# Operands moved to PSUM, and 44 tiles' rows fetched one by one by two DMA queues, in an edge-attention kernel

## The chip, the cores and the metric

One core of one Trainium2 chip runs the kernel. The metric is the device time of one execution in microseconds: 2950.45 us is the median of three runs of the kernel before (2945.25 to 2961.28). Engines are named as in the profile: PE (TensorE, matmuls), PEld (its weight loads), DVE (VectorE), ACT (ScalarE), POOL (GpSimd), SP (SyncE). SP, ACT and POOL also start DMA transfers; "SPq" is SP's instruction queue.

## What is computed

A graph layer with 6250 nodes, 206250 edges sorted by target node, 128 features in 8 heads of 16, all in float32:

```python
Qh = (h @ WQ).reshape(N, H, D)
Kh = (h @ WK).reshape(N, H, D)
Vh = (h @ WV).reshape(N, H, D)
Eh = (edge_attr @ WE).reshape(-1, H, D)
...
score = jnp.einsum('ehd,ehd,ehd->eh', Kh[src], Qh[dst], Eh) * inv_sqrt_d
score = jnp.exp(jnp.clip(score, -5.0, 5.0))
msg = Vh[src] * score[:, :, None]
wV = jax.ops.segment_sum(msg, dst, num_segments=N)
Z = jax.ops.segment_sum(score, dst, num_segments=N)
h_out = wV / (Z[:, :, None] + 1e-06)
...
x = _layernorm(x + h_out.reshape(N, H * D), axis=-1)
```

The costly part is `Kh[src]` and `Vh[src]`: for each edge one row of K and V of a node anywhere in the graph.

## The kernel before, in words

**Tiles and batches.** Edges are cut into 1612 tiles of 128, and four tiles make a batch (`B`, L25). A table `kv` in DRAM holds one row of 1 KB, K beside V, for each node (`table`, L169). The loop at L372 takes one batch per step, in three stages that lie one step apart: `stage_a(b)`, `stage_b(b-1)`, `stage_c(b-2)`. From step 12 on (`XB`) the order of the instructions on each engine is the written one (`manual_schedule`, L374).

**Gathers.** For each tile POOL issues one indirect DMA, which reads 128 rows of `kv` at the node numbers in one column of `src_sb` (`gather`, L251). The first 12 batches gather rows of `x` and project them on the chip (`project`). There are `GB` = 20 batches of gathered rows on the chip, so POOL may run ahead of the arithmetic by about that much. Sixteen tiles are not gathered by POOL: `sp_gather` (L195) lets SP fetch their rows with one DMA for each row, 128 of them spread over 23 steps (`SPN`). For this SP loads 16 node numbers into registers (L210), and then computes an address and starts a DMA for each (L214).

**Arithmetic of a batch.** DVE writes a one-hot matrix of target nodes (`stage_0`, L273: `iota_f` compared with `rel`). PE transposes it (L284) and projects the edge features (L287); ACT copies the transpose from PSUM to SBUF (L289, `onehotT`); PE multiplies it with the window's Q rows (L292). DVE then forms K times Q (L301), times E (L303), sums by head (L306) and clips (L309). ACT takes the exponential (L311) into the last 8 columns of `msg`. One step later DVE multiplies V with it (L331, both operands in SBUF), and PE adds one-hot times messages to the sums of a window (L346). The operands of L273 are both in SBUF as well; L301 and L303 each have one in PSUM.

**Once in 11 tiles.** A new window needs its Q rows: a matmul at L239 and an ACT copy at L241 (`qw`); the finished window's sums go to SBUF by an ACT copy at L356 (`sum`). Once in 33 tiles `finish` (L317) adds windows (L319, copy at L326, `fin`), and a layer norm follows, one DVE instruction at each `fill()`; its store is SP's (L514).

**SP's queue.** In order: one load of edge features for each 8 tiles (512 KB, L226, 6 buffers), the single rows of L214, the loads of `x` (L485) and the stores (L514). Eight semaphores serve the DMAs of SP and ACT in turn; a DMA waits until the one before it on its semaphore has landed.

[...]

Of the kernel before, what the change touches and what calls it, by code (L numbers as in the profile page):

```python
# [9 lines left out]
I32 = mybir.dt.int32  # L10
AF = mybir.ActivationFunctionType
# [20 lines left out]
SPN = 23                       # batches from one tile of SP's rows to the next  # L32
AHEAD = 2                      # batches that the one-hot matrices run ahead
EB = 6                         # edge loads on the chip
SPL = 6                        # batches from the last of its rows to its use
SLAG = 2                       # batches from an output's arithmetic to its store
SPT = list(range(NT - 29, B * (XB + SPN + SPL), -(SPN * B + 1)))[::-1]   # SP's tiles, one DMA a row
SPR = 16                       # indices that SP loads at once


def cut_batches():
    out, t = [], 0
    while t < NT:
        if t in SPT:
            k = 1
        elif t >= NT - TAIL:
            k = 2 if NT - t > 3 else 1
        else:
            stops = [s for s in SPT if s > t] + [NT - TAIL]
            k = min(B, stops[0] - t)  # L50
        out.append(range(t, t + k))
        t += k
    return out

# [17 lines left out]
def edge_attention(ctx: ExitStack, tc: tile.TileContext, x, xT, srcT, srow, dstT, lo, eaT,  # L72
# [23 lines left out]
    shift = cp.tile([P, 3 * P], F32, name="shift")    # shift[i, c] = (c == i + 128)  # L96
# [5 lines left out]
    with ExitStack() as fast:  # L102
# [13 lines left out]
        def relative(a, b):  # L116
            """rel = dst - window start, of tiles a to b"""
            while a < b:
                g = a // G
                if a % G or b - a < G:  # L120
                    e = min(b, (g + 1) * G)
                    nc.vector.tensor_tensor(rel[:, a:e], dst_sb[:, a:e],
                                            lo_sb[:, g:g + 1].to_broadcast([P, e - a]), op=ALU.subtract)
                else:
                    e = b - (b - a) % G
                    k = (e - a) // G
                    nc.vector.tensor_tensor(
                        rel[:, a:e].rearrange("p (g t) -> p g t", t=G),
                        dst_sb[:, a:e].rearrange("p (g t) -> p g t", t=G),
                        lo_sb[:, g:g + k, None].to_broadcast([P, k, G]), op=ALU.subtract)  # L130
# [24 lines left out]
        gp = fast.enter_context(tc.tile_pool(name="gather", bufs=GB))  # L155
        ep = fast.enter_context(tc.tile_pool(name="edges", bufs=EB))
# [33 lines left out]
        batches = cut_batches()  # L190
        nbat = len(batches)
        manual = []
        sp_rows, sp_idx, xbs, stores, norms, pending, ready = {}, {}, {}, [], [], [], []

        def sp_gather(b):  # L195
            """SP's share of the gathers: the rows of tile SPT[i], spread over the batches before it"""
            for i, t in enumerate(SPT):
                at = SPB[i]
                a, e = at - SPN - SPL, at - SPL
                if b == a - 2:  # L200
                    sp_idx[t] = wp.tile([1, P], I32, name="spidx")
                    nc.sync.dma_start(sp_idx[t], srow[:, i * P:i * P + P])
                if not a <= b < e:
                    continue
                r0, r1 = (P * (v - a) // (e - a) for v in (b, b + 1))
                if b == a:
                    sp_rows[t] = wp.tile([P, 1, 2 * D], F32, name="sprows")
                for r in range(r0, r1):
                    if r % SPR == 0:
                        sp_vals[:] = nc.values_load_multi_w_load_instructions(  # L210
                            sp_idx[t][0:1, r:r + SPR], engines=(mybir.EngineType.SP,),
                            min_val=0, max_val=N - 1,
                            skip_runtime_bounds_check_because="src holds node numbers")[1]
                    nc.sync.dma_start(sp_rows[t][r:r + 1, 0, :], kv[ds(sp_vals[r % SPR], 1), :])  # L214

        SPB = [next(b for b, ts_ in enumerate(batches) if ts_[0] == t) for t in SPT]
        sp_vals = []
# [27 lines left out]
        def gather(b):  # L245
            if batches[b][0] in SPT:
                return sp_rows.pop(batches[b][0])
            rows, f = (x, D) if b < XB else (kv, 2 * D)
            g = gp.tile([P, B, 2 * D], F32, name="kvrows")
            for i, t in enumerate(batches[b]):  # L250
                nc.gpsimd.indirect_dma_start(  # L251
                    out=g[:, i, :f], out_offset=None, in_=rows,
                    in_offset=bass.IndirectOffsetOnAxis(ap=src_col(t), axis=0))
            return g

        def project(g, n):
            """K and V rows in the place of gathered x rows"""
# [5 lines left out]
            for i in range(0, n, 2):  # L263
                k = min(2, n - i)
                pk = psT.tile([P, 2, 2 * D], F32, name="kvps", tag="oT")
# [4 lines left out]
        def stage_0(b):  # L270
            t0, n = batches[b][0], len(batches[b])
            oh = wp.tile([P, B, P], F32, name="onehot", bufs=AHEAD + 4)
            nc.vector.tensor_tensor(oh[:, :n], iota_f[:, None, :].to_broadcast([P, n, P]),  # L273
# [24 lines left out]
        def stage_b(b):  # L298
# [10 lines left out]
            nc.vector.tensor_scalar(sc[:, :n], sc[:, :n], -20.0, 20.0, op0=ALU.max, op1=ALU.min)  # L309
            m = wp.tile([P, B, MW], F32, name="msg")  # L310
# [3 lines left out]
        def add_windows(ps, q, stop):  # L314
            """add the sums of the windows that reach into block q"""
# [13 lines left out]
        def stage_c(b):  # L329
            n, g, oh, m = st8.pop(b)  # L330
# [3 lines left out]
                m[:, :n, D:, None].to_broadcast([P, n, H, DH]), op=ALU.mult)  # L334
# [26 lines left out]
        gathered = {b: gather(b) for b in range(min(XB, len(batches)))}  # L361
        for b0 in range(0, NB, KB):
# [3 lines left out]
        def fill():  # L366
            """one step of a layer norm, between the others of VectorE"""
# [4 lines left out]
        for b in range(nbat + 3):  # L372
# [6 lines left out]
            if b < nbat:  # L379
                load_chunk(batches[b][0] // CH + EB - 3)  # L380
                sp_gather(b)
# [37 lines left out]
def any_order(ctx, tc, x, xT_sb, srcT, dstT, eaT, wq_sb, we_sb, iota_f, out, kv, qtab):  # L419
    """The same for edges in any order: each tile of edges is added to every block of nodes."""  # L420
# [68 lines left out]
def layernorm(nc, sp, agg, xb, out, q, stores):  # L489
    """agg: sums of messages and scores of 128 nodes; gives their output rows, an instruction a step"""  # L490
# [14 lines left out]
    # y = (var + eps) ** -0.5: a start from the exponent, then Newton's steps  # L505
# [50 lines left out]
```

## Time and profile before

| what | value |
|---|---|
| median of three runs | 2950.45 us |
| span of the profiled execution, first to last instruction | 2098.6 us |
| median less span | 851.9 us |
| mean granted TensorE clock in it | 0.939 |
| PE, DVE, ACT, POOL busy | 1644.2, 1480.1, 441.4, 1593.3 us |
| DMA traffic | 334.66 MB, mean 159 GB/s |
| HBM read, written | 322.27 MB, 9.60 MB |

The span is that of one profiled execution on the core; the time of the runs also holds what lies before the first and after the last instruction of the program. Busy time is summed over the span, so an engine at 76% may still be the one that all others wait for. A group's row names the line, the engine, the operation, what it writes and reads, the count, then busy time and mean duration, then the idle time of the engine just before these instructions and what ended it.

### The profile page before, as it was taken

How to read it: one execution, taken by the hardware profiler on the slowest of the kernel's cores; microseconds unless marked ns; L12 is line 12 of the kernel's file. 1: busy time of each engine (PE TensorE's matmuls, PEld its weight loads, DVE VectorE, ACT ScalarE, POOL GpSimd, SP SyncE). 2: the span in 40 equal slices, each digit the busy share in tenths (PEclk: the TensorE clock that was granted, in tenths of full speed). 3: DMA queues.
4: the chain of work that ended last, by engine and by line, in shares of the span. 5: the costliest groups of instructions: out<-in, count | busy, mean ns of one | idle time of the engine just before them, and what ended most of it. 6: DMA issues, size and time to landing. Idle time of an engine off the chain costs nothing.

```text
span 2098.6 us, 40013 instructions
## 1 busy us (share of the span) xinstructions
PE 1644.2 (78%) x12306; PEld 1561.1 (74%) x12306; DVE 1480.1 (71%) x3330; ACT 441.4 (21%) x1239; POOL 1593.3 (76%) x1602
## 2 busy tenths in 40 slices
PE   7999787877787677777788777787778777877776
PEld 6899776777777677777787676777767677777766
DVE  3598677777676676777767776767677677766676
ACT  3422121212111121211112122212212121212211
POOL 7777777777777777777777777777777777777775
PEclk9999899999999999999979999989999999899998
DMA  9555455555555455555555455545555555455542
GB/s 313 168 165 177 145 157 153 165 158 150 164 161 162 142 164 158 157 156 152 160 154 169 136 173 159 156 145 166 159 157 155 158 166 158 146 159 149 167 139 79
DMA packets 131782, 334.66 MB, mean 159 GB/s; under 512 B 32790, under 2 KB 54372, under 8 KB 131556
## 3 DMA queue, kind: packets, MB, share of 16 engines
q0 software_dynamic: 75840, 206.15, 33.3%
q1 hardware_dynamic: 54996, 125.45, 19.5%
q8 instruction: 98, 1.61, 0.3%
q14 instruction: 128, 1.05, 0.2%
q10 hardware_dynamic: 720, 0.41, 0.1%
HBM read 322.27 MB, written 9.60 MB: 158 GB/s over the span
## 4 chain that ended last, share of the span: by engine, by line
POOL 30%; DMA 23%; DVE 21%; issue 19%; PE 6%; DVEq 0%; ACT 0%; SPq 0%; POOLq 0%
POOL kvrows L251 30%; DMA kvrows<-kv,src 22%; DVE kq L301 5%; DVE kq L303 5%; DVE sc L306 4%; DVE msg L331 3%; PE agg L346 2%; PE eps L287 2%; PE qps L292 1%; DVE sc L309 1%; PE oTps L284 1%; DVE onehot L273 1%; DVE w L511 0%; PE finps L319 0%; DVEq L301 0%
## 5 line engine op out<-in xcount | busy, mean ns | idle before, releaser
L251 POOL DMA_INDIRECT kvrows<-kv,src x1548 | 1546.2, 999 | 471.7 <-issue 384.9
L346 PE MATMUL agg<-msg,onehot 128*128 128x136 f32 x3224 | 518.6, 306 | 424.2 <-DVE msg L331 389.1
L346 PEld LDWEIGHTS agg<-msg,onehot 128*128 128x128 f32 x3224 | 438.8, 204 | 481.2 <-DVE msg L331 479.6
L301 DVE TENSOR_TENSOR kq<-kvrows,qps 128x512 f32<-128x512 f32 (+1 forms) x402 | 274.4, 682 | 542.1 <-DMA kvrows<-kv,src 450.7
L292 PE MATMUL qps<-qw,onehotT 128*128 128x128 f32 x3224 | 476.9, 291 | 3.3 <-ACT onehotT L289 2.6
L287 PE MATMUL eps<-we_sb,ea 128*128 128x128 f32 x3224 | 461.5, 289 | 0.0
L287 PEld LDWEIGHTS eps<-we_sb,ea 128*128 128x128 f32 x3224 | 429.5, 207 | 0.1
L292 PEld LDWEIGHTS qps<-qw,onehotT 128*128 128x128 f32 x3224 | 405.6, 197 | 18.3 <-ACT onehotT L289 9.2
L289 ACT COPY onehotT<-oTps 128x512 f32<-128x512 f32 (+2 forms) x418 | 238.6, 571 | 644.5 <-PE oTps L284 641.3
L306 DVE TENSOR_REDUCE sc<-kq 128x32 f32<-128x512 f32 (+2 forms) x418 | 278.3, 666 | 9.4
L303 DVE TENSOR_TENSOR kq<-kq,eps 128x512 f32<-128x512 f32 (+2 forms) x418 | 278.6, 667 | 7.5
L273 DVE TENSOR_TENSOR onehot<-iota_f,rel 128x512 f32<-128x512 f32 (+2 forms) x418 | 277.4, 664 | 0.0
L331 DVE TENSOR_TENSOR msg<-kvrows,msg 128x512 f32<-128x512 f32 (+1 forms) x402 | 274.2, 682 | 4.0 <-ACT msg L311 3.9
L284 PE MATMUL oTps<-shift,onehot 128*128 128x128 f32 x1612 | 271.3, 294 | 0.0
L284 PEld LDWEIGHTS oTps<-shift,onehot 128*128 128x128 f32 x1612 | 213.8, 153 | 2.5 <-ACT kvrows L268 2.1
L311 ACT ACTIVATE msg<-sc 128x32 f32<-128x32 f32 (+2 forms) x418 | 95.9, 229 | 468.5 <-DVE sc L309 466.5
L309 DVE TENSOR_SCALAR sc<-sc 128x32 f32<-128x32 f32 (+2 forms) x418 | 82.9, 198 | 9.5
L241 ACT COPY qw<-qwps 128x128 f32<-128x128 f32 x147 | 39.2, 267 | 217.0 <-PE qwps L239 216.8
L356 ACT COPY sum<-agg 128x136 f32<-128x136 f32 x146 | 39.7, 272 | 148.1 <-PE agg L346 146.3
L319 PE MATMUL finps<-sum,shift 128*128 128x136 f32 x478 | 64.5, 283 | 0.0
L319 PEld LDWEIGHTS finps<-sum,shift 128*128 128x128 f32 x478 | 59.9, 193 | 0.0
L251 POOL DMA_INDIRECT kvrows<-x,src x48 | 46.3, 964 | 16.5 <-issue 14.3
(50 smaller groups left out, 437.5 us busy)
## 6 DMA issues: line engine op xcount, KB each, us to landing
ea<-eaT SPq DMA_DIRECT2D x201, 512.0 KB
sprows<-kv SPq DMA_DIRECT2D x2048, 1.0 KB
kvrows<-kv,src POOLq DMA_INDIRECT x1548
kv<-kvst SPq DMA_DIRECT2D x12, 512.0 KB
xb<-x SPq DMA_DIRECT2D x48, 64.0 KB
out<-h SPq DMA_DIRECT2D x48, 64.0 KB
xT_sb<-xT SPq DMA_DIRECT2D x5, 535.0 KB
kvrows<-x,src POOLq DMA_INDIRECT x48
```

The lines of the kernel that those rows point to most:

```text
L251: nc.gpsimd.indirect_dma_start(out=g[:, i, :f], out_offset=None, in_=rows, in_offset=bass.IndirectOffsetOnAxis(ap=src_col(t), axis=0))
L273: nc.vector.tensor_tensor(oh[:, :n], iota_f[:, None, :].to_broadcast([P, n, P]), rel[:, t0:t0 + n, None].to_broadcast([P, n, P]), op=ALU.i ...
L284: nc.tensor.transpose(oT[:, i, :], oh[:, i, :], ident)
L287: nc.tensor.matmul(pe[:, i, :], ea_tile(t0 + i), we_sb, start=True, stop=True)
L289: nc.scalar.copy(ohT[:, :n], oT[:, :n])
L292: nc.tensor.matmul(pq[:, i, :], ohT[:, i, :], window_q(*group_of(t0 + i)), start=True, stop=True)
L301: nc.vector.tensor_tensor(t1[:, :n], g[:, :n, :D], pq[:, :n], op=ALU.mult)
L303: nc.vector.tensor_tensor(t1[:, :n], t1[:, :n], pe[:, :n], op=ALU.mult)
L306: nc.vector.tensor_reduce(sc[:, :n], t1[:, :n].rearrange("p b (h d) -> p b h d", h=H), axis=AX.X, op=ALU.add)
L319: nc.tensor.matmul(ps, shift[:, P - s:2 * P - s], sums[k], start=i == 0, stop=stop and i == len(parts) - 1)
L331: nc.vector.tensor_tensor(m[:, :n, :D].rearrange("p b (h d) -> p b h d", h=H), g[:, :n, D:].rearrange("p b (h d) -> p b h d", h=H), m[:, : ...
L346: nc.tensor.matmul(aggs[k], oh[:, i, :], m[:, i, :], start=first and not final, stop=last)
```

## The change

Two operands move to PSUM. A new PSUM bank holds `iota_p`, a copy of `iota_f` that is made once, and `exp_p`, 32 columns for one batch of exponentials. The one-hot comparison reads `iota_p`. The exponential is taken twice by ACT, into `exp_p` and into the columns of `msg`; the product with V reads `exp_p`. For the bank, `psT` goes from two buffers to one, and the products of `project` go to `psE` and `psQ`. The exponentials move behind the next one-hot comparison in the written order, and `stage_c` is split into `messages` and the rest.

Eleven batches of four tiles are fetched row by row, in place of sixteen tiles: 336 of a batch's 512 rows by SP and 176 by ACT, spread over 33 steps that end 4 steps before the batch's own. The steps 12 to 374 hold such rows, some 10 on SP and 5 or 6 on ACT in each step; ACT's stand at the end of a step, behind its exponentials and its `sum` copy and ahead of the next step's `onehotT` copy. Node numbers are loaded once and multiplied by 1024 once, on DVE; each register load still brings 16 of them, and each DMA takes its address from a register as it is, as bytes. POOL gathers 1568 tiles (1596 before), the last of them without its padding. All batches but the last few have four tiles now (406 batches, 418 before). `GB` goes from 20 to 18, `SLAG` from 2 to 4 (steps from an output's arithmetic to its store).

```diff
-GB = 20                        # batches of gathered rows on the chip
+GB = 18
...
-SLAG = 2                       # batches from an output's arithmetic to its store
+SLAG = 4
+RN = 33
+RL = 4
+RSP = 336
+RV = 16
+RBYTES = 4 * 2 * D
...
+ROWB = list(range(XB + RN + RL, len(BATCHES) - TAIL, RN))
...
+        off_sb = ip.tile([len(ROWB), B * P], I32, name="off_sb")
...
+        def row_offsets():
+            nc.scalar.dma_start(off_sb, srow)
+            nc.vector.tensor_scalar(off_sb, off_sb, float(RBYTES), None, op0=ALU.mult)
...
-        psT = fast.enter_context(tc.tile_pool(name="psT", bufs=2, space=bass.MemoryType.PSUM))
+        psT = fast.enter_context(tc.tile_pool(name="psT", bufs=1, space=bass.MemoryType.PSUM))
...
+        psX = fast.enter_context(tc.tile_pool(name="psX", bufs=1, space=bass.MemoryType.PSUM))
+        bank = psX.tile([P, P + B * H], F32, name="bank")
+        iota_p, exp_p = bank[:, :P], bank[:, P:].rearrange("p (b h) -> p b h", h=H)
+        nc.vector.tensor_copy(iota_p, iota_f)
...
+        def single_rows(b, queue):
+            for i, at in enumerate(ROWB):
+                a, e = at - RN - RL, at - RL
                 if not a <= b < e:
                     continue
+                if at not in row_tiles:
+                    row_tiles[at] = hp.tile([P, B, 2 * D], F32, name="hwrows")
+                first, last = (0, RSP) if queue is nc.sync else (RSP, B * P)
+                r0, r1 = (first + (last - first) * (v - a) // (e - a) for v in (b, b + 1))
+                engine = mybir.EngineType.SP if queue is nc.sync else mybir.EngineType.Activation
                 for r in range(r0, r1):
+                    if (r - first) % RV == 0:
+                        vals[engine] = nc.values_load_multi_w_load_instructions(
+                            off_sb[i:i + 1, r:r + RV], engines=(engine,),
...
-                    nc.sync.dma_start(sp_rows[t][r:r + 1, 0, :], kv[ds(sp_vals[r % SPR], 1), :])
+                    queue.dma_start(row_tiles[at][r % P:r % P + 1, r // P, :].bitcast(U8),
+                                    kv_bytes[None, ds(vals[engine][(r - first) % RV], RBYTES)])
...
-            nc.vector.tensor_tensor(oh[:, :n], iota_f[:, None, :].to_broadcast([P, n, P]),
+            nc.vector.tensor_tensor(oh[:, :n], iota_p[:, None, :].to_broadcast([P, n, P]),
...
+        def weigh(b):
+            n, g, oh, sc = st8[b]
+            nc.scalar.activation(exp_p[:, :n], sc[:, :n], AF.Exp, scale=0.25)
             m = wp.tile([P, B, MW], F32, name="msg")
             nc.scalar.activation(m[:, :n, D:], sc[:, :n], AF.Exp, scale=0.25)
...
+        def messages(b):
+            n, g, oh, m = st8[b]
             nc.vector.tensor_tensor(
                 m[:, :n, :D].rearrange("p b (h d) -> p b h d", h=H),
                 g[:, :n, D:].rearrange("p b (h d) -> p b h d", h=H),
-                m[:, :n, D:, None].to_broadcast([P, n, H, DH]), op=ALU.mult)
+                exp_p[:, :n, :, None].to_broadcast([P, n, H, DH]), op=ALU.mult)
...
             if 0 <= b - 1 < nbat:
                 stage_b(b - 1)
             if 0 <= b - 2 < nbat:
-                stage_c(b - 2)
+                messages(b - 2)
             fill()
             if b + AHEAD < nbat:
                 stage_0(b + AHEAD)
+            if 0 <= b - 1 < nbat:
+                weigh(b - 1)
+            if 0 <= b - 2 < nbat:
+                stage_c(b - 2)
             fill()
+            single_rows(b, nc.scalar)
```

More of the change, by code (lines that the diff above doesn't have):

```diff
@@ L10 @@
 I32 = mybir.dt.int32
+U8 = mybir.dt.uint8
 AF = mybir.ActivationFunctionType
@@ L31 @@
 NG = (NT + G - 1) // G
-SPN = 23
 AHEAD = 2
 EB = 6
-SPL = 6
-SLAG = 2
-SPT = list(range(NT - 29, B * (XB + SPN + SPL), -(SPN * B + 1)))[::-1]
-SPR = 16
+SLAG = 4
[4 more added lines that the diff above has]
+RBYTES = 4 * 2 * D
 def cut_batches():
@@ L43, in cut_batches @@
     while t < NT:
-        if t in SPT:
-            k = 1
-        elif t >= NT - TAIL:
+        if t >= NT - TAIL:
             k = 2 if NT - t > 3 else 1
         else:
-            stops = [s for s in SPT if s > t] + [NT - TAIL]
-            k = min(B, stops[0] - t)
+            k = min(B, NT - TAIL - t)
         out.append(range(t, t + k))
@@ L53, in cut_batches @@
     return out
+BATCHES = cut_batches()
+ROWB = list(range(XB + RN + RL, len(BATCHES) - TAIL, RN))
 def group_of(t):
@@ L155, in edge_attention @@
         gp = fast.enter_context(tc.tile_pool(name="gather", bufs=GB))
+        hp = fast.enter_context(tc.tile_pool(name="rows", bufs=2))
         ep = fast.enter_context(tc.tile_pool(name="edges", bufs=EB))
@@ L188, in table @@
                 nc.sync.dma_start(kv[b * P:N], st[:N - b * P, b - b0, :])
-        batches = cut_batches()
+        batches = BATCHES
         nbat = len(batches)
         manual = []
[L193 to L202, printed above, removed]
+        xbs, stores, norms, pending, ready = {}, [], [], [], []
@@ L203, in sp_gather @@
+        row_tiles, vals = {}, {}
+        kv_bytes = kv.bitcast(U8).rearrange("n f -> (n f)")
+        def single_rows(b, queue):
+            for i, at in enumerate(ROWB):
+                a, e = at - RN - RL, at - RL
                 if not a <= b < e:
                     continue
-                r0, r1 = (P * (v - a) // (e - a) for v in (b, b + 1))
-                if b == a:
-                    sp_rows[t] = wp.tile([P, 1, 2 * D], F32, name="sprows")
+                if at not in row_tiles:
[3 more added lines that the diff above has]
+                engine = mybir.EngineType.SP if queue is nc.sync else mybir.EngineType.Activation
@@ L208, in sp_gather @@
                 for r in range(r0, r1):
[L209 to L212, printed above, removed]
+                    if (r - first) % RV == 0:
+                        vals[engine] = nc.values_load_multi_w_load_instructions(
+                            off_sb[i:i + 1, r:r + RV], engines=(engine,),
+                            min_val=0, max_val=(N - 1) * RBYTES,
@@ L213, in sp_gather @@
                             skip_runtime_bounds_check_because="src holds node numbers")[1]
-                    nc.sync.dma_start(sp_rows[t][r:r + 1, 0, :], kv[ds(sp_vals[r % SPR], 1), :])
-        SPB = [next(b for b, ts_ in enumerate(batches) if ts_[0] == t) for t in SPT]
-        sp_vals = []
+                    queue.dma_start(row_tiles[at][r % P:r % P + 1, r // P, :].bitcast(U8),
+                                    kv_bytes[None, ds(vals[engine][(r - first) % RV], RBYTES)])
         chunks, qw, aggs, sums, st8 = {}, {}, {}, {}, {}
@@ L245, in gather @@
         def gather(b):
-            if batches[b][0] in SPT:
-                return sp_rows.pop(batches[b][0])
+            if b in ROWB:
+                return row_tiles.pop(b)
             rows, f = (x, D) if b < XB else (kv, 2 * D)
@@ L250, in gather @@
             for i, t in enumerate(batches[b]):
+                k = min(P, E - t * P + 1)
+                if k < P:
+                    nc.vector.memset(g[:, i, :], 0.0)
                 nc.gpsimd.indirect_dma_start(
-                    out=g[:, i, :f], out_offset=None, in_=rows,
-                    in_offset=bass.IndirectOffsetOnAxis(ap=src_col(t), axis=0))
+                    out=g[:k, i, :f], out_offset=None, in_=rows,
+                    in_offset=bass.IndirectOffsetOnAxis(ap=src_col(t)[:k], axis=0))
             return g
@@ L264, in project @@
                 k = min(2, n - i)
-                pk = psT.tile([P, 2, 2 * D], F32, name="kvps", tag="oT")
+                pk = (psE, psQ)[i // 2 % 2].tile([P, 2, 2 * D], F32, name="kvps", tag=("eps", "qps")[i // 2 % 2])
                 for j in range(k):
@@ L309, in stage_b @@
             nc.vector.tensor_scalar(sc[:, :n], sc[:, :n], -20.0, 20.0, op0=ALU.max, op1=ALU.min)
+            st8[b] = [n, g, oh, sc]
+        def weigh(b):
+            n, g, oh, sc = st8[b]
+            nc.scalar.activation(exp_p[:, :n], sc[:, :n], AF.Exp, scale=0.25)
             m = wp.tile([P, B, MW], F32, name="msg")
@@ L327, in finish @@
             pending.append(layernorm(nc, sp, fin, xbs.pop(q), out, q, stores))
-        def stage_c(b):
-            n, g, oh, m = st8.pop(b)
+        def messages(b):
+            n, g, oh, m = st8[b]
             nc.vector.tensor_tensor(
@@ L333, in stage_c @@
                 g[:, :n, D:].rearrange("p b (h d) -> p b h d", h=H),
-                m[:, :n, D:, None].to_broadcast([P, n, H, DH]), op=ALU.mult)
+                exp_p[:, :n, :, None].to_broadcast([P, n, H, DH]), op=ALU.mult)
+        def stage_c(b):
+            n, g, oh, m = st8.pop(b)
             for i in range(n):
@@ L361, in edge_attention @@
         gathered = {b: gather(b) for b in range(min(XB, len(batches)))}
+        row_offsets()
         for b0 in range(0, NB, KB):
@@ L380, in edge_attention @@
                 load_chunk(batches[b][0] // CH + EB - 3)
-                sp_gather(b)
+                single_rows(b, nc.sync)
                 g = gathered.pop(b) if b in gathered else gather(b)
@@ L536 @@
         "srow": np.ascontiguousarray(np.concatenate(
-            [srcT[t * P:t * P + P] for t in SPT or [0]])[None]),
+            [srcT[BATCHES[b][0] * P:][:B * P][None] for b in ROWB])),
         "dstT": np.ascontiguousarray(dstT.reshape(NT, P).T),
```

## The prediction, made before the changed kernel ran

> **What bounds the kernel now.** I read first the busy times, the chain that ended last, and the costliest group.
>
> ```profile
> PE 1644.2 (78%) x12306; PEld 1561.1 (74%) x12306; DVE 1480.1 (71%) x3330; ACT 441.4 (21%) x1239; POOL 1593.3 (76%) x1602
> ...
> POOL 30%; DMA 23%; DVE 21%; issue 19%; PE 6%; DVEq 0%; ACT 0%; SPq 0%; POOLq 0%
> ...
> L251 POOL DMA_INDIRECT kvrows<-kv,src x1548 | 1546.2, 999 | 471.7 <-issue 384.9
> ```
>
> No engine is busy over 78%, yet POOL's idle time is "issue": it waits for nothing. In the timeline of POOL, the pause between two gathers is 0.30 us each time:
>
> ```profile
> 1007.94 0.95 POOL L251 DMA_INDIRECT kvrows<-kv,src  x1 [0.30 <-issue]
> 1009.19 0.95 POOL L251 DMA_INDIRECT kvrows<-kv,src  x1 [0.30 <-issue]
> 1010.45 1.13 POOL L251 DMA_INDIRECT kvrows<-kv,src  x1 [0.31 <-DVE msg L331]
> 1011.88 0.94 POOL L251 DMA_INDIRECT kvrows<-kv,src  x1 [0.30 <-issue]
> ```
>
> So POOL works end to end: its 1596 gathers start on average 1.302 us apart, from 3.7 us to 2082.2 us. Without disturbance one costs 0.95 + 0.30 = 1.25 us; the rest is stretched gathers like that of 1.13 us. In the timeline of DVE the stretched one lies on the two instructions that read two operands from SBUF:
>
> ```profile
> 1009.47 0.69 DVE L331 TENSOR_TENSOR msg<-kvrows,msg 128x512 f32<-128x512 f32 x1
> 1010.07 0.69 DVE L273 TENSOR_TENSOR onehot<-iota_f,rel 128x512 f32<-128x512 f32 x1
> ```
>
> The waits say who suffers, and the windows say what the rest could do:
>
> ```profile
> DVE kq L301 <- DMA kvrows<-kv,src: 450.7, 268, 4.2
> ACT qw L241 <- PE qwps L239: 216.8, 142, 2.9
> ACT sum L356 <- PE agg L346: 146.3, 124, 2.9
> ...
> 110.00:190.00 80.00, 77.55 (x646) 74.99 (x644) 77.74 (x180) 20.93 (x61) 61.70 (x61) 1.00 0.57 172
> ```
>
> DVE waits 450.7 us for gathered rows. From 110 to 190 us, where POOL is still ahead, DVE is busy 77.74 of 80 us and a batch takes (193.9 - 108.5) / 23 = 3.7 us, from the starts of L301 in batches 12 and 35. Later a batch takes the gathers' 4 x 1.30 = 5.2 us.
>
> **POOL's part of the change.** Of the gathers 292 take over 1.0 us; all time above 948 ns sums to 79 us. In the 277 of them after the hundredth, L273 covers 499 ns on average and L331 222 ns, against 52 and 129 ns in the short ones. Both read only one operand from SBUF afterwards. The gain lies between 0 (the overlap is chance) and 79 us. I take 60: L273 and L331 make three quarters of DVE's time in the long ones, and the layer norm's own two-operand instructions stay. DVE's rows give no reason for a price of its own: L303, with a PSUM operand, takes 686 ns, L273 683 ns. [...]
>
> Twenty-eight fewer gathers at 1.25 us give 35 us. POOL would end 95 us sooner, at 1987 us; with the 16.4 us from the last gather to the end the span is 2003, and with the 851.9 us outside it, kept as they are, 2855 us.
>
> **SP's and ACT's part.** A step of 4 tiles then has 32/33 x 4 x 1.26 = 4.9 us of POOL time (1.25 us and the 20 us of stretching left over 1568 gathers). In it SP must start 336/33 = 10.2 rows and ACT 5.3. A row costs SP now 0.41 us from start to start: 37 ns of address arithmetic, a 29 ns move and the 228 ns DMA instruction, with pauses. Afterwards it is 0.28 (DMA and its pause) to 0.34 us (the move stays). A register load took 1.23 us for 16 indices, so 0.79 us per step on SP and 0.41 on ACT; edge loads, x and stores add 0.3. SP needs 10.2 x 0.28 + 1.1 = 3.9 to 4.6 us: nearly full, with 4.9 as its limit.
>
> The eight semaphores are the doubtful point. A row lands 1.35 to 3.1 us after its issue (10th to 90th percentile; median 1.87, mean 2.10, from the semaphore records of L214), an edge load 3.97 us. The written program gives the semaphores out in turn over both queues, with ACT's rows between SP's. So no DMA starts before the eighth before it, from either queue, has landed. Before, eight rows took SP 8 x 0.41 = 3.3 us, which covered the landing, and only edge loads were waited for (29.1 us in 61 waits). Now 16.3 DMAs a step (512/33 rows, 0.5 edge loads, 0.25 for x and stores) at 1.87 us over 8 semaphores need 3.8 us with no gap at all, and while the queues alternate a pair costs 1.87 / 4 = 0.47 us.
>
> What is behind ACT's rows matters: the next step's `onehotT` copy, for which PE's L292 waits, then L346, then DVE's L301. ACT's time per step when it is not waiting for gathers: copy 0.57 + 0.09 of pauses, two exponentials at 0.23 + 0.1, `qw` with its wait for PE (216.8/142 + 0.27 = 1.8 us) and `sum` with its own (1.45 us), both 147 times in 406 batches, 1.17 us a step. That makes 2.4 us. Rows: 5.33 x 0.47 = 2.5 and 0.41 of register loads. Sum: 5.3 us a step. From both sides: 2.4 + 5.33 x 0.28 + 0.41 = 4.3 if no DMA waits (then POOL's 4.9 rules), and 3.7 + 2.9 = 6.6 if the rows stand wholly behind the work of the dense stretch. I take 5.3, because in steps with `qw` and `sum` ACT starts no row for some 3 us, in which SP gets 8 DMAs further and stops. [...]
>
> The span then: step 12 at 108 us as before, 363 steps with rows, 31 batches at 3.7 us (gathers for 18 are already there), 12 us from the last L301 to the end: 108 + 363p + 115 + 12 = 235 + 363p. No change at p = (2098.6 - 235) / 363 = 5.13. With p = 5.3 it is 2159 us, 60 more than before. Against the median: 2950.45 + 60 = 3010 us. With p = 5.8, 3192.
>
> **Edits at nothing.** The second exponential (406 x 0.23 = 93 us of ACT) is counted above. Copies of `iota_p`, the multiplication of addresses and one load lie in the first 100 us, where POOL runs ahead and needs nothing. With one `psT` buffer, and projections in `psE` and `psQ`, each of the first 12 batches may wait for a copy more: 0 to 12 x 0.6 = 7 us, hidden by the 39 us that POOL is ahead at step 12, but added to the sum where POOL doesn't bound. `SLAG` takes away SP's waits for L513 (563.6 us), of which nobody was waiting for the end. `GB` 18 only shortens a lead of 2 batches out of 20.
>
> **The rivals.**
> 1. (0.44) The forecast: the shared semaphores and ACT's order bound the steps, p = 5.3, 3010 us. For it: the landing times against 8 semaphores. Against it: ACT is busy 21%, and in before SP's waits for DMAs are small. In a part of this case, some 0.07, p lies within 0.04 of 5.13 and the time stays.
> 2. (0.36) The other side: DMA waits stay under 0.3 us a step, POOL bounds as before, with fewer and unstretched gathers: 2855 us (2832 with all 79 us). It decides when p is under 4.9: a row on ACT for 0.39 us or less (2.4 + 5.33 x 0.39 + 0.41 = 4.9).
> 3. (0.15) SP is the bound: the move stays, edge loads hold a semaphore (3.97 us against 2.5 us for a turn of eight, 1.5 us every second step) and register loads are not hidden: 4.6 + 0.75 + 0.5 = 5.85 us, 2359 us of span, 3210 us. The edge loads then come late and PE waits at L287.
> 4. (0.05) The move to PSUM does nothing, POOL bounds: only 35 us, 2915 us.
>
> **How the numbers follow.** Slower by over 0.5% (15 us, about what a measurement of this kernel can tell from no change): 0.37 of case 1 and all of case 3, 0.52. Faster: cases 2 and 4, 0.41. Same: 0.07. The time is that of case 1, 3010 us; its own range is 2950 to 3190 (p 5.13 to 5.8). The range has to take in case 2 as well: 2842 to 3190; a tenth lies below or just at its lower edge, and a tenth above, most of case 3.
>
> **What would show it.** Right: gathers of L267 with a mean near 0.96 us, but POOL waiting for buffers; ACT's rows 0.45 us or more apart; PE's L308 of the changed kernel waiting for ACT's `onehotT`; SP's row DMAs waiting for DMAs of ACT. Wrong: DVE's first product still waits for gathered rows with POOL in an even beat of 1.25 us up to about 1970 us; then case 2 holds. If gathers stay stretched on the one-hot comparison (its line 289), the PSUM part failed. An edge load that ends PE's wait at L303 is case 3. A median less span other than 852 us would break the addition.

## The result, and the profile after

The changed kernel takes 3249.24 us (median of 4 runs, 3248.23 to 3249.48). The kernel before, run beside it, takes 2947.85 us (2916.09 to 2961.28). The ratio is 1.1035, with a 95% interval of 1.0961 to 1.1109: slower by a tenth. The prediction was slower, at 3010 us with 3190 as its upper end, so the side is right and the size far too small.

The runs were made on several chips, and the kernel before takes 2883 to 2948 us on some and 2099 to 2102 us on others, so each ratio below is against the kernel before on the same chip, and each section says which kind it was.

The profiled execution of the changed kernel has a span of 3246.4 us, with 3248.23 us as its time. First the page (busy times, granted clock, costliest groups):

```profile
PE 1939.0 (60%) x12306; PEld 1828.6 (56%) x12306; DVE 1467.8 (45%) x3261; ACT 466.0 (14%) x1621; POOL 1488.9 (46%) x1574
...
PEclk6798778778778777887877887777787787787789
...
L267 POOL DMA_INDIRECT kvrows<-kv,src x1520 | 1442.3, 949 | 1725.1 <-DVE msg L353 765.7
L303 PE MATMUL eps<-we_sb,ea 128*128 128x128 f32 x3224 | 567.9, 332 | 748.8 <-DMA ea<-eaT 722.0
```

POOL worked end to end before, with 999 ns a gather. Now a gather takes 949 ns, and POOL idles 1725.1 us before these gathers. The largest part, 765.7 us, ends with DVE's `msg` (L353), that is, with the reading of a buffer of gathered rows. So the gathers became cheaper and stopped being the limit. The waits say who is late:

```profile
DVE kq L317 <- PE qps L308: 959.4, 189, 11.8
POOL kvrows L267 <- DVE msg L353: 765.7, 135, 10.8
...
PE eps L303 <- DMA ea<-eaT: 722.0, 145, 10.3
ACT onehotT L305 <- PE oTps L300: 538.8, 108, 12.8
ACT onehotT L305 <- DMA hwrows<-kv: 433.0, 183, 11.0
```

and the waits of SP's queue (us in total, times, longest):

```profile
SPq L229 <- DMA hwrows<-kv: 453.4, 290, 14.2
```

Before, DVE waited for gathered rows, and PE not for edge features (0.0 us idle before its L287). Now PE waits 722 us for edge loads (`ea`), which SP issues; DVE waits behind PE, and POOL behind DVE. And SP itself waits 453.4 us in the middle of its rows for other row transfers. A step of four tiles takes (3133.4 - 742.3) / 300 = 7.97 us, from the starts of L317 in batches 80 and 380.

The kernel's own profile of before (span 2098.6 us) came from an execution of the quicker kind. The same changed kernel, profiled where the kernel before takes 2101 us (run e15), can therefore be set against it line by line:

```profile
PE 1799.1 (66%) x12306; PEld 1717.4 (63%) x12306; DVE 1467.5 (53%) x3261; ACT 469.9 (17%) x1621; POOL 1484.9 (54%) x1574
...
PE 37%; DMA 34%; SPq 10%; DVE 6%; issue 6%; ACTq 5%; ACT 3%; DVEq 0%
DMA ea<-eaT 20%; PE qps L308 12%; DMA hwrows<-kv 12%; PE eps L303 12%; SPq L229 7%; PE agg L371 6%; ACTq L229 3%; PE finps L341 2%; SPq L225 2%; PE oTps L300 2%; DVE kq L319 1%; DVE kq L317 1%; ACT onehotT L305 1%; DVE sc L322 1%; PE qwps L252 1%
...
L267 POOL DMA_INDIRECT kvrows<-kv,src x1520 | 1438.5, 946 | 1228.7 <-DVE msg L353 518.4
```

In the chain that ended last POOL had 30%; now it has no share at all. The chain runs through edge loads (20%), PE, the single rows (12%) and the queues of SP and ACT (10% and 5%), which had none.

### The profile page after: what moved, and what is told of

Read it like the earlier page. It is cut to its first block, busy times and chain, and to the rows that moved or that the text cites. A ratio compares the mean times of both kernels' runs of the same rounds, so it can differ in the third digit from the quotient of the medians.

```text
span 3246.4 us, 45133 instructions
## 1 busy us (share of the span) xinstructions
PE 1939.0 (60%) x12306; PEld 1828.6 (56%) x12306; DVE 1467.8 (45%) x3261; ACT 466.0 (14%) x1621; POOL 1488.9 (46%) x1574
## 5 line engine op out<-in xcount | busy, mean ns | idle before, releaser
L267 POOL DMA_INDIRECT kvrows<-kv,src x1520 | 1442.3, 949 | 1725.1 <-DVE msg L353 765.7
L303 PE MATMUL eps<-we_sb,ea 128*128 128x128 f32 x3224 | 567.9, 332 | 748.8 <-DMA ea<-eaT 722.0
L303 PEld LDWEIGHTS eps<-we_sb,ea 128*128 128x128 f32 x3224 | 506.9, 239 | 787.0 <-DMA ea<-eaT 758.1
L317 DVE TENSOR_TENSOR kq<-kvrows,qps 128x512 f32<-128x512 f32 (+1 forms) x395 | 269.3, 682 | 1479.0 <-PE qps L308 959.4
L308 PE MATMUL qps<-qw,onehotT 128*128 128x128 f32 x3224 | 589.6, 341 | 306.8 <-ACT onehotT L305 154.2
L308 PEld LDWEIGHTS qps<-qw,onehotT 128*128 128x128 f32 x3224 | 529.0, 248 | 342.7 <-ACT onehotT L305 179.9
L305 ACT COPY onehotT<-oTps 128x512 f32<-128x512 f32 x406 | 236.8, 583 | 1506.8 <-PE oTps L300 538.8
L300 PE MATMUL oTps<-shift,onehot 128*128 128x128 f32 x1612 | 272.8, 296 | 130.2 <-ACT qw L254 57.0
L300 PEld LDWEIGHTS oTps<-shift,onehot 128*128 128x128 f32 x1612 | 214.8, 156 | 142.5 <-ACT qw L254 63.4
L322 DVE TENSOR_REDUCE sc<-kq 128x32 f32<-128x512 f32 x406 | 276.6, 681 | 9.1
L319 DVE TENSOR_TENSOR kq<-kq,eps 128x512 f32<-128x512 f32 x406 | 276.6, 681 | 7.4
L353 DVE TENSOR_TENSOR msg<-kvrows,bank 128x512 f32<-128x512 f32 (+1 forms) x395 | 267.4, 677 | 21.7 <-issue 11.9
L289 DVE TENSOR_TENSOR onehot<-bank,rel 128x512 f32<-128x512 f32 x406 | 275.7, 679 | 0.0
L333 ACT ACTIVATE msg<-sc 128x32 f32<-128x32 f32 x406 | 88.1, 217 | 0.1
```

The lines of the kernel that those rows point to most:

```text
L267: nc.gpsimd.indirect_dma_start(out=g[:k, i, :f], out_offset=None, in_=rows, in_offset=bass.IndirectOffsetOnAxis(ap=src_col(t)[:k], axis=0))
L289: nc.vector.tensor_tensor(oh[:, :n], iota_p[:, None, :].to_broadcast([P, n, P]), rel[:, t0:t0 + n, None].to_broadcast([P, n, P]), op=ALU.i ...
L300: nc.tensor.transpose(oT[:, i, :], oh[:, i, :], ident)
L303: nc.tensor.matmul(pe[:, i, :], ea_tile(t0 + i), we_sb, start=True, stop=True)
L305: nc.scalar.copy(ohT[:, :n], oT[:, :n])
L308: nc.tensor.matmul(pq[:, i, :], ohT[:, i, :], window_q(*group_of(t0 + i)), start=True, stop=True)
```

## The experiments

### One part at a time, where the kernel before takes 2883 us

**e1: the PSUM part alone.** The kernel before, with its 16 tiles on SP, and the two operands moved, with what goes with them: the second exponential, its place behind the next one-hot comparison, and one `psT` buffer. The main lines:

```diff
+        bank = psX.tile([P, P + B * H], F32, name="bank")
+        iota_p, exp_p = bank[:, :P], bank[:, P:].rearrange("p (b h) -> p b h", h=H)
-            nc.vector.tensor_tensor(oh[:, :n], iota_f[:, None, :].to_broadcast([P, n, P]),
+            nc.vector.tensor_tensor(oh[:, :n], iota_p[:, None, :].to_broadcast([P, n, P]),
...
-                m[:, :n, D:, None].to_broadcast([P, n, H, DH]), op=ALU.mult)
+                exp_p[:, :n, :, None].to_broadcast([P, n, H, DH]), op=ALU.mult)
```

> Only the operands in PSUM, with the order of the exponentials and one psT buffer; SP's 16 tiles as before. Theory (the rows are what costs, PSUM helps POOL): gathers at a mean of 0.95 us instead of 1.00 and 40 to 80 us less than before, a ratio of 0.973 to 0.987. Rival (the new order and the single psT buffer cost the time): a ratio of 1.03 or more, with ACT or PE waiting for the other.

Measured: 2981.87 us, ratio 1.0393 [1.0262, 1.0524]. The gathers fall to 947 ns, and the time does not:

```profile
L255 POOL DMA_INDIRECT kvrows<-kv,src x1548 | 1465.5, 947 | 1372.3 <-DVE msg L340 581.0
```

POOL idles 1372.3 us, for the most part behind DVE (581.0 us behind `msg` alone), so on this chip the gathers are not the limit, and what a cheaper gather is worth can't be read here.

**e2: the changed kernel with one batch fetched singly instead of eleven.**

```diff
-ROWB = list(range(XB + RN + RL, len(BATCHES) - TAIL, RN))
+ROWB = list(range(XB + RN + RL, len(BATCHES) - TAIL, 33 * 40))
```

> The changed kernel with one batch fetched row by row instead of eleven; POOL gathers the other 1608 tiles. Theory: without rows on SP and ACT a batch takes POOL's 5.0 us, a ratio near 0.985 to 1.0. Rival (something else of the change, SLAG or GB or PSUM, is slow): near the changed kernel's 1.10.

Measured: 2864.2 us, 0.9965 [0.9914, 1.0015], against 1.10 for eleven batches. The PSUM operands, the byte addresses and the new order of the exponentials are all in this kernel, so the loss comes with the single rows.

**e3: all 512 rows of a fetched batch on SP, none on ACT.**

```diff
-RSP = 336
+RSP = 512
```

> The changed kernel with all 512 rows of a batch on SP's queue and none on ACT's. Theory (two queues that share eight semaphores hold each other, and ACT's compute stands behind its rows): SP alone needs 15.5 rows x 0.34 us + 1.2 us of register loads + 0.3 = 6.8 us a step, less than the 7.9 us now, so faster than the changed kernel, a ratio of 0.9 to 1.02 to before. Rival (SP's own stream is the bound and ACT relieves it): slower than the changed kernel, a ratio of 1.15 or more.

Measured: 3386.53 us, 1.1784 [1.1664, 1.1904]. This is the rival's side, not the theory's. SP now issues 15.5 rows a step; its waits for other rows come to 63.5 us only, and yet PE waits 1066.8 us at L303 for edge loads. Between batches 80 and 380 SP's instructions, with the pauses of up to 0.1 us between them, take 6.7 us of a step of 8.5, more than the 4.9 us that POOL needs. So too many rows on one queue cost as well, with no row of ACT on the semaphores: SP's own issue is the limit there. That alone doesn't say which of the two holds in the changed kernel, with 10.2 rows a step.

### Where the kernel before takes 2099 us

**e4: the kernel before, profiled once.** 

> The kernel before, unchanged, for a profile beside the others of this call: its timed runs took some 2880 us, its first profile 2098.6. Theory: its span is now near its timed runs, and shows the same pauses of 5 to 9 us, in which ACT waits for PE, as the changed kernel and the two with few rows; POOL then isn't at work end to end. Rival: its span is near 2100 us again, and 800 us lie outside the span.

Measured: 2102.43 us, with a span of 2100.6. The span is near the run's time, as the theory had it, but both are near 2100 us, which neither side had: little lies outside the span.

**e5: the kernel before without single rows** (`SPT = []`), so that POOL gathers 16 tiles more.

> The kernel before with no tile fetched by SP: POOL gathers all 1612 tiles. Theory (POOL is not the bound in the timed runs, and rows on SP cost and don't help): a ratio of 0.96 to 0.995. Rival (POOL bounds, as in the first profile): 16 more gathers of 1.25 us, a ratio of 1.007 or more.

Measured: 2119.63 us, 1.0092 [1.0062, 1.0122]. Sixteen gathers at the prediction's 1.302 us are 20.8 us; the difference is 20.6. On this chip POOL is the limit of the kernel before, as its profile said.

**e6: 66 steps for a fetched batch instead of 33** (`RN = 66`: five batches, 5.1 rows a step on SP and 2.7 on ACT).

> The changed kernel with a batch's rows spread over 66 steps instead of 33: 5 batches of 512 rows, half as many rows in a step on both queues. Theory (the queues are full and hold each other on eight semaphores only at the full rate): 8.5 DMAs a step wait for little, a ratio of 0.99 to 1.02. Rival (each row costs the same, wherever it stands): 5 of 11 batches cost 2048 of 5120 rows' 0.107, a ratio of 1.03 to 1.05.

**e7: 256 rows of each of the 11 batches on SP, none on ACT**, the other two tiles gathered by POOL:

```diff
-RSP = 336
+RSP = 256
...
+            if b in ROWB:
+                g = row_tiles.pop(b)
...
+                if b in ROWB and i < RSP // P:
+                    continue
...
-            single_rows(b, nc.scalar)
```

> The changed kernel with 256 rows of a batch on SP, none on ACT, and the batch's other two tiles gathered by POOL. Theory (ACT's rows and the shared semaphores are the cost): SP needs 7.8 x 0.45 + 0.6 + 0.4 = 4.5 us a step and isn't the bound, a ratio of 0.99 to 1.02. Rival (each row costs the same): half of the rows, a ratio of 1.04 to 1.06.

Measured: e6 2019.12 us, 0.9613 [0.9587, 0.9639]; e7 2016.29 us, 0.9599 [0.9572, 0.9625]. Both are 4% faster than before, and POOL is the limit in both: e6's 1592 gathers at 1.25 us and some 25 us around them make 2015. With fewer rows, or with rows on one queue, nothing is lost.

### Again, where the kernel before takes 2948 us

**e8: the changed kernel. e9: e1's kernel. e10: e3's. e11: 44 steps for a batch** (`RN = 44`: eight batches, 7.6 rows a step on SP and 4 on ACT).

> The changed kernel once more, to be read against the kernel before on the same chip, which took 2099 us in the last call and some 2880 to 2950 us in the ones ahead of it. Where before takes about 2099 us: theory A (the shared semaphores and ACT's order bind, 5.1 us a step or more): 2090 us or more, a ratio of 1.0 to 1.05. Theory B (POOL bounds with 1568 gathers of 1.25 us): 3 + 1960 + 16 = 1980 us, a ratio of 0.943. Where before takes about 2900 us: 1.10 again.

> Only the operands in PSUM, as in e1. Where before takes about 2099 us: theory (two SBUF operands hold POOL up): 1596 gathers of 1.25 us, 2015 us, a ratio of 0.96. Rival (no gain from PSUM alone; the 4% gained by the two runs of the last call came from rows): 0.99 or more. Where before takes about 2900 us: 1.04 again.

> All 512 rows of a batch on SP, as in e3. Where before takes about 2099 us: theory (SP's stream is then the bound): 15.5 x 0.33 + 1.2 + 0.4 = 6.7 us a step, 235 + 363 x 6.7 = 2667 us, a ratio of 1.2 to 1.3. Rival (rows are hidden wherever they stand): 0.95. Where before takes about 2900 us: 1.18 again.

> The changed kernel with a batch's rows spread over 44 steps: 8 batches, 32 tiles. Where before takes about 2099 us: 1580 gathers, 3 + 1975 + 16 = 1994 us, a ratio of 0.95 if POOL bounds; above 0.96 if the queues still bind at 7.6 rows a step on SP and 4 on ACT. Where before takes about 2900 us: between 1.0 and 1.10.

Measured: e8 3255.98 us, 1.1038 [1.0949, 1.1127]; e9 3018.32 us, 1.0253 [1.017, 1.0335]; e10 3443.27 us, 1.1683 [1.1592, 1.1773]; e11 3038.13 us, 1.0289 [1.0196, 1.0382]. From one batch over eight to eleven the ratio climbs from 0.9965 (e2, on another chip) over 1.029 to 1.104, steeper at the end; the 1.029 can't be told from e9's 1.025, which has none of these rows. In e11 the waits of SP's rows for other rows are as long as in the changed kernel (499.6 us against 469.9 in e8), but PE's waits for edge loads are a third (260.4 us against 737.3): so long waits alone don't make the loss.

### Taking the two queues apart, where the kernel before takes 2101 us

**e12: SP's 336 rows kept, ACT's 176 given back to POOL** (a whole tile, and the first 48 rows of the tile that SP fetches in part):

```diff
+SKIP = 3 * P - RSP
...
+                    w = r + SKIP * (r >= 2 * P)
...
+                if b in ROWB and i < 2:
+                    continue
+                k = SKIP if b in ROWB and i == 2 else min(P, E - t * P + 1)
...
-            single_rows(b, nc.scalar)
```

> The changed kernel with ScalarE's 176 rows of each fetched batch given back to POOL (the last tile whole, and 48 rows of the tile before it), and SP's 336 rows kept. SP so issues 10.1 rows a step as before, but shares the transfers' semaphores with no row of ScalarE. Theory (SP is held back by semaphores that ScalarE's rows issued late hold, 422.8 us of 2400 in the trace of the changed kernel, and while it waits the edge loads queue behind it): SP's waits behind ScalarE's rows are gone, PE's waits for edge loads at L303 fall from 722 us to under 150, and where the kernel before takes some 2900 us the ratio is 0.98 to 1.04; where it takes 2099 POOL sets the time, 1590 gathers x 1.25 + 25 = 2013 us, ratio 0.96. Rival (the number of rows on SP alone makes the time): SP still has no rest, L303 still waits over 500 us for edge loads, and the ratio is 1.06 to 1.10 where before takes 2900 and above 0.98 where it takes 2099.

**e13: e7's kernel beside it.** 

> The kernel of e7 again, beside the others on one chip: 256 rows of each of the 11 batches on SP, 7.8 a step, none on ScalarE, the other two tiles on POOL. Where before takes some 2900 us: 0.97 to 1.03 by either theory; by the theory of shared semaphores it stands within 0.02 of e12, by the rival of row numbers it is lower than e12 by 0.03 or more. Where before takes 2099: 0.96 as in e7.

**e14: e6's kernel beside it.** 

> The kernel of e6 again, beside the others on one chip: five batches fetched singly over 66 steps each, so 5.1 rows a step on SP and 2.7 on ScalarE, semaphores still shared. Both theories: SP has time left over at this rate. Where before takes some 2900 us: 0.99 to 1.03, on the line from one batch (0.9965) to eight (1.029) and eleven (1.104). If it stands above e13 though SP issues a third fewer rows in it, the shared semaphores cost by themselves. Where before takes 2099: 0.96 as in e6.

**e15: the changed kernel beside them.** 

> The changed kernel as it is, beside the others on one chip. Where before takes some 2900 us: 1.10 again. Where it takes 2099 (not yet measured for this kernel): if POOL set the time there, 1568 gathers x 1.25 + 25 = 1985 us, ratio 0.946; by the prediction's order, 5.3 us a step over 363 steps, 2159 us, ratio 1.03; if SP sets it, 10.1 rows x 0.34 + 0.71 of register loads + 0.33 of edge loads = 4.5 us a step before any wait for a shared semaphore, and with the 1.9 us a step of such waits 6.4 us, 235 + 363 x 6.4 = 2558 us, ratio 1.22.

| run | rows a step on SP / ACT | time, us | ratio [95%] |
|---|---|---|---|
| e12 | 10.2 / 0 | 2015.52 | 0.9590 [0.9574, 0.9606] |
| e13 | 7.8 / 0 | 2016.27 | 0.9591 [0.9574, 0.9608] |
| e14 | 5.1 / 2.7 | 2018.28 | 0.9606 [0.9590, 0.9622] |
| e15 | 10.2 / 5.3 | 2749.12 | 1.3093 [1.3057, 1.3129] |

e12 and e15 differ in ACT's 176 rows of eleven batches, 1936 transfers, for which e12 has 22 gathers more on POOL; the transfers cost 734 us. SP's number of rows is not the cause by itself at this rate (e12 equals e13). Where the gathers set the time of the kernel before, the changed kernel loses 31%, three times the loss of the result. Here the expectation for SP as the limit (6.4 us a step, 2558 us) was too small too.

In e12 POOL runs without a wait again, DVE waits for gathered rows, PE no more for edge loads, and SP's rows at most for the edge loads on their semaphores. In this order the page, the waits of the engines, and the largest wait of SP's queue:

```profile
L272 POOL DMA_INDIRECT kvrows<-kv,src x1520 | 1442.1, 949 | 467.2 <-issue 368.0
```

```profile
DVE kq L322 <- DMA kvrows<-kv,src: 320.8, 209, 4.7
```

```profile
SPq L231 <- DMA ea<-eaT: 125.8, 109, 2.4
```

and in e15, the waits of the engines and of SP's queue:

```profile
DVE kq L317 <- PE qps L308: 1023.4, 291, 9.9
...
PE eps L303 <- DMA ea<-eaT: 708.8, 156, 8.4
ACT onehotT L305 <- PE oTps L300: 596.1, 141, 11.2
ACT onehotT L305 <- DMA hwrows<-kv: 592.1, 237, 11.1
```

```profile
SPq L229 <- DMA hwrows<-kv: 752.0, 495, 10.4
```

Set side by side by step (between batches 80 and 380), SP's instructions, with the pauses of up to 0.1 us between them, take 4.49 us a step in e12 and the same 4.49 us in e15. The longer pauses, in which SP waits, take 0.44 us in e12's step of 4.94 us and 2.54 us in e15's step of 7.03 us. So the whole difference is waiting. Going by the semaphore of each transfer, 988 of SP's rows in this stretch have a row of ACT just before them on their semaphore. Of these 306 waited, for 584.3 us in all: 1.95 us a step, nearly the 2.1 that e15 has above e12. In 117 cases SP arrived before ACT had begun to issue its row; these make 415.1 us, 219.0 us of it until ACT issued the row and the rest until it landed. The other 189 waited 169.2 us for a row on its way.

How the wait feeds itself shows in 17 us of e15's timeline (start, duration, engine, line, count, and the idle time before with its releaser; POOL's and DVE's lines left out):

```profile
1363.91 0.38 SPq L239 DMA_DIRECT2D ea<-eaT  x1
1364.39 16.25 SPq L229 DMA_DIRECT2D hwrows<-kv  x21
1364.89 3.64 ACTq L229 DMA_DIRECT2D hwrows<-kv  x5
...
1367.67 2.07 PE L303 MATMUL eps<-we_sb,ea 128*128 128x128 f32 x8 [6.44 <-DMA ea<-eaT]
...
1373.06 0.95 PE L300 MATMUL oTps<-shift,onehot 128*128 128x128 f32 x4
...
1374.05 0.59 ACT L305 COPY onehotT<-oTps 128x512 f32<-128x512 f32 x1 [10.18 <-PE oTps L300]
...
1377.11 1.92 ACTq L229 DMA_DIRECT2D hwrows<-kv  x5
...
1380.73 0.36 SPq L239 DMA_DIRECT2D ea<-eaT  x1
```

SP issues an edge load at 1363.91, so late that PE stands still for 6.4 us until it is there. PE's next transposes (L300) come behind that, so ACT's copy waits 10.18 us for them, and ACT's rows of that step, which stand behind the copy in ACT's queue, start at 1377.11. SP had started 17 of its 21 rows by 1373.04. Its next has the semaphore of ACT's second row, which is issued at 1377.44; SP goes on at 1378.98, 5.9 us after its last row. Behind those rows stands SP's next edge load, issued at 1380.73, again late. SP waits for ACT, ACT for PE, PE for SP's edge load: that is a loop.

What closes the loop so tightly, by this trace, is the order in which the semaphores were given out. In the written program SP loads edge features six steps ahead of their use, so SP could be some steps late at no price. But each queue issues its rows in the written order, 336 and 176 of them in 33 steps, so the step of each row can be counted. In 1086 of the 1208 places in e15 where a row of SP stands right behind a row of ACT on its semaphore, ACT's row belongs to a step that comes 5 or 6 later in the written program (1087 of 1209 in the result's trace). Above, the row of SP that waits until 1378.98 is of step 193, and the row of ACT that it waits for is of step 199; the edge load behind it, SP's of step 194, is for step 200. So SP mostly can't finish a step before ACT is five or six steps further on, and the lead of the edge loads is used up.

e14 shows that such waits need not cost anything. There SP waits for other single rows 629.8 us in all, against 752.0 in e15. But with 5 rows a step its own work is 2.3 us (between batches 20 and 340, counted as above), and its waits of 2.5 us fit into the rest of POOL's 4.9. The edge loads are on time. Two things differ from e15, though. Besides the rows being half as many a step, the row of ACT before a row of SP is of a step anywhere from six earlier to three later. e11 has nearly the order of e15 (838 of 945 are 4 to 6 steps later) with three quarters of the rows a step, and PE's waits were a third there, so the number of rows counts too. No run kept the rows of the changed kernel and changed the order of the semaphores, or gave each queue its own, so how much of the 31% is the order's is not shown.

### The other half, and the gain, where the kernel before takes 2102 us

**e16: ACT's 176 rows kept, SP's 336 given back to POOL.**

```diff
+                if b in ROWB and i == 3:
+                    continue
+                k = RSP - 2 * P if b in ROWB and i == 2 else min(P, E - t * P + 1)
...
-                single_rows(b, nc.sync)
```

> The counterpart of e12: ScalarE's 176 rows of each of the 11 batches are kept as in the changed kernel (5.3 a step), and SP's 336 rows are given back to POOL (two tiles whole, and 80 rows of the third). ScalarE now shares the semaphores with SP's few loads of edges only. Theory (each queue alone bears its rows; it is the two together that hold each other up): POOL sets the time, 1601 gathers x 1.25 + 25 = 2026 us, ratio 0.965 where the kernel before takes 2100 us; 0.97 to 1.05 where it takes 2900. Rival, the step of the prediction (ScalarE's own rows fill its step: 2.4 us of work + 2.5 of rows + 0.4 of register loads = 5.3 us a step): 235 + 363 x 5.3 = 2159 us, ratio 1.03 where before takes 2100, and PE waits for ScalarE's onehotT; if rows on ScalarE cost more than that, up to the 1.31 of the changed kernel.

**e17: e1's kernel again.** 

> The kernel of e1 and e9 again: the kernel before with the two operands in PSUM and its 16 tiles of single rows left as they were. On the chips where before takes 2900 us it stood at 1.025 to 1.039. Where before takes 2100: the gathers fall from 0.999 to 0.948 us and POOL sets the time, 1596 x 1.25 + 25 = 2020 us, ratio 0.962, so that all that e12, e13 and e14 gained is PSUM's and nothing the rows'. Rival (the rows of before, at 128 a tile on few steps, hold something up): 0.98 or more.

**e18: e12's kernel again.** 

> The kernel of e12 again, beside e16 and e17 on one chip. Where before takes 2100: 0.959 as before, 2013 us. Where it takes 2900 (not yet measured): 0.98 to 1.04 if the shared semaphores are what costs there too, 1.06 to 1.10 if SP's number of rows is.

Measured: e16 2029.22 us, 0.9650 [0.9634, 0.9666]; e17 2019.93 us, 0.9606 [0.9590, 0.9622]; e18 2016.73 us, 0.9591 [0.9575, 0.9607].

ACT's rows do disturb ACT in e16, as the waits show, and cost nothing:

```profile
ACT onehotT L308 <- DMA hwrows<-kv: 630.6, 288, 4.2
POOL kvrows L270 <- issue: 390.4, 1281, 0.3
...
PE qps L311 <- ACT onehotT L308: 327.7, 290, 2.8
...
DVE kq L320 <- DMA kvrows<-kv,src: 211.1, 121, 4.3
```

ACT's copy stands 630.6 us behind its rows and PE 327.7 us behind the copy, but never longer than 4.2 and 2.8 us, and the step takes 4.90 us: POOL waits for nothing ("issue"), and sets the time. So SP's rows alone are free, ACT's alone are free, and the two together cost a third. e17 says where the 4% of e12 to e16 comes from: the kernel before with only its two operands in PSUM gets 0.9606 of e12's 0.959. The more rows that e12, e13 and e14 fetch singly are worth no more than those of the 16 tiles that SP fetched before.

```profile
L255 POOL DMA_INDIRECT kvrows<-kv,src x1548 | 1466.2, 947 | 471.7 <-issue 378.8
```

e12 is faster than both kernels where the kernel before takes 2100 us: 4.1% below it and 27% below the changed one (2015.52 against 2749.12). How e12 and e16 do where the kernel before takes 2900 us was not tried.

## Why the prediction was wrong

**The step that failed** is the one that priced the shared semaphores: "while the queues alternate a pair costs 1.87 / 4 = 0.47 us", put on ACT's rows, with "5.3 us a step" for ACT and a span of 2159. The doubtful point was the right one, but it was charged to ACT, and SP's sum (3.9 to 4.6 us) was given no wait for it. The runs show the reverse. ACT's rows start 0.33 us apart in the median, in the result, e15 and e16 alike, and ACT with all its rows needs no more than the 4.90 us of e16's step. SP's own work is 4.49 us a step in e12 and e15, as predicted, but in e15 SP waits another 1.95 us a step behind rows of ACT, and the step takes 7.03 us. In the result SP works 4.7 us and stands still for 3.3 of a step of 7.97.

An average landing time at an even turn of the queues couldn't give this price, for two reasons. Of the 584.3 us, 219.0 us are no landing time: SP stands before a semaphore whose row ACT has not issued, because ACT has work between its rows. And "ACT's rows between SP's" is true of the semaphores only with a shift: the rows of ACT there are mostly of a step 5 or 6 later. That the edge loads would lose their lead by it was not in the forecast's sum.

That the time moved to the side that was forecast is in part luck: the mechanism that was named is at work, but the 60 us come from a sum for ACT, which bounds nothing. Of the signs named, SP's rows waiting for ACT's and POOL waiting for buffers came; ACT's rows 0.45 us or more apart did not; and the sign of case 3, an edge load that ends PE's wait at L303, did.

**The rivals.** Rival 3 named what the trace shows, edge loads late and PE waiting at L303, and its 3210 us is within 1.2% of the result. That nearness is luck: its price was made of other things, 0.75 us for edge loads that hold a semaphore and 0.5 for register loads, and in e12, which has both, there is no loss. Its span of 2359 us is far from e15's 2746.1; only as a difference added to the median did it come near. Rival 2 (POOL bounds) is true as soon as either queue is left out.

**PSUM.** Predicted 60 us, between 0 and 79. e17 against the kernel before is 2102.49 - 2019.93 = 82.6 us, and (999 - 947) ns x 1548 = 80: the upper end, so the stretching by instructions with two operands in SBUF was all there was to gain (e17 also has the new order of the exponentials and one `psT` buffer, for which the sum leaves nothing). In the result nothing of this gain is left, as POOL no longer sets the time.

**POOL as the limit, 1.302 us a gather and 1.25 undisturbed:** right where the kernel before takes 2100 us (e5: 20.6 us for 16 gathers; e12 to e14 and e16 to e18: time = gathers x 1.25 + 25, within 5 us). The 2832 us of rival 2 should have been 2836, 19 below its 2855.

**Fewer gathers, 35 us:** never collected, since the kernel that has them is bound elsewhere.

**SP's rows:** 0.28 to 0.34 us predicted. 0.32 is the median from row to row in e12 and e15, so the move stays (29 ns in e15), as the upper end had it, and the sum's upper end of 4.6 us is near the 4.49 us that SP works. "Nearly full" was right.

**The formula** 235 + 363p gives 2787 us with e15's 7.03; its span is 2746.1. The form was right, p was not.

**851.9 us outside the span:** this addition was wrong. In every run here the time is some 2 us above the span (3248.23 and 3246.4 in the result, 2102.43 and 2100.6 in e4). The profile of before simply came from an execution of the other kind. A difference that large between a profile's span and the times should have been read as two conditions, and the step's price carried over as a range for both.

**Open.** Why the kernel before takes 2900 us on some chips and 2100 on others. On the former POOL is not its limit even with cheap gathers (e1 waits for DVE), and PE stands still for over 3 us at a time 151 times, for 940 us in all (e1's trace, against 19 times and 67 us in e4's), at a granted clock of 0.80 against 0.94; what causes these stops was not found, nor why e1 and e9 are 2.5 to 3.9% slower there with cheaper gathers. So for the result itself, a loss of 10%, the shared semaphores are shown as a wait (578.3 us of SP's behind rows of ACT between 400 and 2800 us of its trace, 201.7 us of it before ACT had issued them; the 422.8 us in e12's expectation are its waits behind late rows, landing included), but not by removing them there; the removal was shown where the loss is 31%.

## What to carry to other kernels

Two queues that take their completion semaphores from one set held each other up here (ratio 1.3093 in e15), though each alone cost nothing (0.9590 in e12, 0.9650 in e16): the queue with little else to do waited for the one with the busy engine (584.3 us of SP's behind rows of ACT in e15). Before spreading small transfers over two queues, look at which semaphores they would share, in which order the compiled program gives them out (here a row behind one of five or six steps later), and at what stands behind them in the queue that will wait (here the edge loads, which closed a loop). Try each queue alone first: one of them may be enough, and a part that gains (the operands in PSUM) can be taken without the part that loses.

## What the runs showed of the hardware that was not expected

Two queues issued transfers at the same time. In e15 315 rows of ACT start within 0.1 us of one of SP's: the longer of each such pair takes 228 ns in the median and 278 at the 90th percentile, and a row alone 228. If one had waited for the other's whole instruction, one of a pair would take some 456 (an estimate, 2 x 228); a shorter wait within the 228 is not excluded. A few rows do take over 400 ns, but not because of the other queue: ACT has 122 of them among its 1936 rows in e15, and 123 in e16, where SP fetches none. So it is the semaphores that tied one queue to the other, as far as these runs show.
